# A graph layer on one core: bins made two blocks ahead, count matmuls first in a block, the last three tiles behind two groups of sums

## The chip, the core and the metric

The kernel runs on one core of one Trainium2 chip. The metric is device microseconds of one execution; the time before is the median of seven runs. A profile is one execution under the hardware profiler. Its engines are TensorE (PE, with its weight loads PEld), VectorE (DVE), ScalarE (ACT), GpSimd (POOL) and SyncE (SP), which issues most DMA transfers.

## What is computed

One message-passing layer over a graph of 6250 nodes and 206250 edges, sorted in the reference by `dst`; the kernel sums by `src`. Cut to what matters:

```python
msg  = concat([x[dst], edge_attr], 1)             # 64 + 64 features per edge
h    = relu(msg @ W1a.T + b1a)                    # 128 per edge
h    = h @ W1b.T + b1b                            # 64 per edge
sums = segment_sum(h, src, 6250); counts = segment_sum(1, src, 6250)
agg  = sums / max(counts, 1)
z    = relu(concat([x, agg], 1) @ W2a.T + b2a) @ W2b.T + b2b
y    = x + concat([z, x], 1) @ Wr.T + br
out  = layernorm(y)
```

## The kernel before

The edges are cut into 124 blocks of 13 tiles of 128 edges (`NGR`, `BLK`). A block goes through these steps; the line numbers are those of the kernel before.

- **Loads (`group`, SyncE).** The edge features (line 700) and the block's dst numbers relative to a window (`relt`, line 886) go into one of `EDGES` = 4 `rhs` buffers; 64 rows of the node table `ytab` go into `mv` (line 892).
- **`columns` (VectorE, line 898).** One comparison makes a one-hot of the dst numbers in the lower half of `rhs`.
- **`hidden` (TensorE, ScalarE).** 13 matmuls (line 912; in float32 each is two passes in the trace) into three PSUM buffers `h_ps`, in parts of 4, 3, 3 and 3 tiles, and a relu of each part (line 913) into one of `ROWS` = 6 `orow` buffers. Before the relus ScalarE writes the low bits of the src numbers into the same buffer (the "lo copy", line 1149), and for that the scatters that last read this buffer must have landed.
- **`bins_of` (VectorE, lines 811 to 818).** For each tile it marks which of 49 bins of 128 nodes each edge belongs to (`bins`) and counts the earlier ones by a scan (`had`). Each block continues the scan of the block before.
- **`counts_of` (TensorE, lines 831 and 832).** Four matmuls turn `bins` and `had` into places, in the only PSUM buffer `cnt_ps`.
- **`slots` (VectorE, lines 848 and 853).** A maximum over the bins and one more operation give `rowidx`, the row in DRAM for each edge.
- **`scatter` (GpSimd, line 919).** 13 indirect DMAs write the block's rows of `orow` to their places in `rows`, which is sorted by bins of nodes.
- **Sums.** From time to time a step's finished part of `rows` is read back: `issue` reads groups of at most three bins with up to 9 buffers `rt` (line 968, SyncE); `sum_next` makes a one-hot `oh` of the nodes (lines 994 and 997, VectorE) and multiplies (line 1015, TensorE), one group at a time, and adds an earlier group into `part` (line 1073). A read waits until the step's last block has landed; a step's reads begin four blocks after its end. `due` is the number of groups that are waiting to be summed when a block begins.

Blocks fall into five epochs (82, 17, 14, 7 and 4 blocks) with a buffer of rows each in turn. In the loop the order on TensorE, ScalarE, VectorE and SyncE is the program's order; GpSimd issues scatters alone. After the loop come the sums of the step before the last, and then, in an order made by a scheduler, the last step's sums and the node work, four bins at a time (lines 1225 to 1276).

In a block `k` the order was: bins of `k + 1`; loads of `k + 3`; the lo copy; the first ten tiles; reads; counts of `k + 1`; one group of sums; the last three tiles; the scatter; slots of `k + 1`; the other groups of sums; columns of `k + 2`.

Of the kernel before, what the change touches and what calls it, by code (L numbers as in the profile page):

```python
# [17 lines left out]
P = 128  # L18
# [440 lines left out]
SUMS, TILES = 3, 14  # L459
SEG = 25  # L460
PRE = 6
ROWS, EDGES, READS = 6, 4, 9
SPREAD = 4.8
EARLY = 14
CLEAR = 4
# [10 lines left out]
def fast_path(  # L476
# [201 lines left out]
    part = const.tile([P, NB, H + 1], F32, name="part")  # L678
    with (
        tc.tile_pool(name="orow", bufs=1) as op,  # L680
        tc.tile_pool(name="oh", bufs=2) as ohp,
        tc.tile_pool(name="node", bufs=4) as nodep,
        tc.tile_pool(name="cps", bufs=1, space=PSUM) as cpp,
        tc.tile_pool(name="slotp", bufs=1, space=PSUM) as slpp,
# [109 lines left out]
        def tiles_of(lo, hi_):  # L794

            t0 = lo
            while t0 < hi_:
                n = -(-(hi_ - t0) // -(-(hi_ - t0) // RD))
                yield t0, n
                t0 += n  # L800

        def bins_of(k):


            ep_ = epoch_of[k]
            c0 = k * BLK
            oh = slp.tile([P, 2 * HALF * T], BF16, name="bins")
            had = slp.tile([P, 2 * HALF * T], BF16, name="had")
            by_bin = oh.rearrange("p (b t) -> p b t", t=T)
            was = none_b if k == ep_.first else state["had"][:, :, BLK]  # L810
            nc.vector.tensor_tensor(by_bin[:, :, 0], was, on.rearrange("p (b t) -> p b t", t=T)[:, :, 1], op=ALU.mult)  # L811
            nc.vector.tensor_tensor(  # L812
                by_bin[:, :, 1:],
                ramp[:, : 2 * HALF, None].to_broadcast([P, 2 * HALF, BLK]),
                hi[:, None, c0 : c0 + BLK].to_broadcast([P, 2 * HALF, BLK]),
                op=ALU.is_equal,
            )
            nc.vector.tensor_tensor_scan(had, on, oh, 0.0, op0=ALU.mult, op1=ALU.add)  # L818
            oh, had = (v.rearrange("p (b t) -> p b t", t=T) for v in (oh, had))
            state["had"] = had  # L820
            return oh, had

        def counts_of(oh, had):
# [11 lines left out]
        def slots(k, ps):  # L835

            ep_ = epoch_of[k]
            c0 = k * BLK
            at = (k - ep_.first) % SEG * BLK
            if at == 0:  # L840
                m = min(ep_.end - k, SEG) * BLK
                state["bin"] = slp1.tile([P, SEG * BLK], F32, name="bin_at")[:, :m]
                nc.vector.tensor_scalar(
                    state["bin"], hi[:, c0 : c0 + m], float(STRIDE), -BIG, op0=ALU.mult, op1=ALU.add
                )
            v = ps[:, :, : HALF * T].rearrange("p i (b t) -> p i b t", t=T)
            row = slp.tile([P, T], F32, name="row")
            nc.vector.tensor_reduce(row, v.rearrange("p i b t -> p t i b"), axis=mybir.AxisListType.XY, op=ALU.max)  # L848

            def by_now(t):  # L850
                nc.vector.tensor_copy(t.rearrange("p (i b) -> p i b", i=2), v[:, :, :, BLK])

            s = nc.vector.scalar_tensor_tensor(
                rowidx[:, c0 : c0 + BLK], row[:, :BLK], BIG + STRIDE - 1,
                state["bin"][:, at : at + BLK], op0=ALU.min, op1=ALU.add,
            )
            state["slots"] = s.ins
            if k + 1 == EARLY:
                by_now(early)
                wrong(early, epochs[0].low, ALU.is_gt, slp)  # L860
            for st in ep_.steps[:-1]:
                if k + 1 == st.at:
                    full = slp1.tile([P, 2 * HALF], F32, name="full")
                    by_now(full)
                    wrong(full, st.hi, ALU.is_lt, slp)
            if k + 1 == ep_.end:
                by_now(ep_.tot)
                unused(ep_)

                if (ep_.end - ep_.first) * BLK > 255:  # L870
                    most = slp.tile([P, 2 * HALF], F32, name="most")
                    nc.vector.tensor_scalar(
                        most, state["had"][:, :, BLK], 255.5, None, op0=ALU.is_gt, op1=ALU.add,
                        accum_out=bad[:, state["bad"] :][:, :1],
                    )
                    state["bad"] += 1
# [18 lines left out]
        def columns(g):  # L895

            rhs, rel, _ = made[g]
            nc.vector.tensor_tensor(  # L898
                rhs[D:, :].rearrange("p (h e) -> p h e", h=2), rel,
                in_win[D:, :, None].to_broadcast([WIN, 2, NG * P // 2]), op=ALU.is_equal,  # L900
            )
# [3 lines left out]
        def hidden(k, parts):  # L905
            orow = orows[k % ROWS]
            rhs, _, m = made[k]
            for k0, n in parts:
                ps = hp.tile([P, SUB, H], F32, name="h_ps")
                for j in range(n):  # L910
                    c = k0 + j
                    nc.tensor.matmul(ps[:, j, :], rhs[:, c * P : (c + 1) * P], m, start=True, stop=True)  # L912
                nc.scalar.activation(orow[:, k0 : k0 + n, :H], ps[:, :n, :], AF.Relu)  # L913
# [224 lines left out]
        slots(0, counts_of(*bins_of(0)))  # L1138
        columns(0)
        columns(1)  # L1140
        for k, ep_ in enumerate(epoch_of):
            if k + 1 < NGR:
                ahead = bins_of(k + 1)

            if k + 3 < NGR:
                made[k + 3] = group(k + 3)
            due = len(issued) + len(marked) + len(to_issue)
            to_issue += groups_at[k]
            nc.scalar.copy(orows[k % ROWS][:, :, H + 1], lo[:, k * BLK : (k + 1) * BLK])  # L1149
            hidden(k, ((0, 4), (4, 3), (7, 3)))  # L1150
            if k == 0:
                bins(HEAD, NT)
                for i, o in enumerate((ALU.min, ALU.max)):
                    nc.vector.tensor_reduce(out_of[:NGR, i : i + 1], rel, axis=mybir.AxisListType.X, op=o)
            if k == 1:
                wn1b, wn2b = load(w1b, "wn1b"), load(w2b, "wn2b")
                b1b_c, b2b_c = column(b1b, "b1b_c"), column(b2b, "b2b_c")
                w2x_t = const.tile([D + 1, H], F32, name="w2x_t")
                nc.sync.dma_start(w2x_t[:D, :], w2aT[:D])
                nc.sync.dma_start(w2x_t[D:, :], b2a.rearrange("(o p) -> o p", o=1))  # L1160
                w2m_t = load(w2aT[D:], "w2m_t")
                wrz_t = load(wrT[:D], "wrz_t")
                wrx_t = const.tile([D + 1, D], F32, name="wrx_t")
                nc.sync.dma_start(wrx_t[:D, :], wrT[D:])
                nc.sync.dma_start(wrx_t[D:, :], br.rearrange("(o p) -> o p", o=1))
            if k == 4:


                wps = slpp.tile([P, P], F32, name="cnt_ps")
                nc.tensor.matmul(wps, wn1b, w2m_t, start=True, stop=True)  # L1170
                wam_t = const.tile([P, P], F32, name="wam_t")
                nc.vector.tensor_copy(wam_t, wps)
                wps = slpp.tile([P, D], F32, name="cnt_ps")
                nc.tensor.matmul(wps, wn2b, wrz_t, start=True, stop=True)
                wzz_t = const.tile([P, D], F32, name="wzz_t")
                nc.vector.tensor_copy(wzz_t, wps)
                nwzz_t = const.tile([P, D], F32, name="nwzz_t")
                nc.vector.tensor_scalar(nwzz_t, wps, -1.0, None, op0=ALU.mult)
                wps = slpp.tile([P, H + D], F32, name="cnt_ps")
                nc.tensor.matmul(wps[D : D + 1, :H], b1b_c, w2m_t, start=True, stop=True)  # L1180
                nc.tensor.matmul(wps[D : D + 1, H:], b2b_c, wrz_t, start=True, stop=True)
                nc.vector.tensor_add(w2x_t[D:, :], w2x_t[D:, :], wps[D : D + 1, :H])
                nc.vector.tensor_add(wrx_t[D:, :], wrx_t[D:, :], wps[D : D + 1, H:])
                nc.vector.tensor_add(wrx_t[:D, :], wrx_t[:D, :], ident[:D, :D])
            if 0 <= k - PRE < -(-NB // SUB):
                nodes_ahead((k - PRE) * SUB)
            if k in clears:
                clear(*clears[k])
            issue(k)
            if k + 1 < NGR:  # L1190
                ahead = counts_of(*ahead)

            if due > 0:
                sum_next()
                issue(k)
            hidden(k, ((10, 3),))
            made.pop(k)
            scatter(ep_, k)
            if k + 1 < NGR:
                slots(k + 1, ahead)  # L1200
            for _ in range(due - 1):
                sum_next()
                issue(k)
            if due == 0:
                collect(0)
            if k + 2 < NGR:
                columns(k + 2)
        for k in range(NGR, NGR + LATE):
            to_issue += groups_at[k]
            issue(k)  # L1210
# [164 lines left out]
```

## Time and profile before

| what | us |
|---|---|
| median of seven runs (lowest, highest) | 2213.67 (2211.32, 2215.72) |
| the profiled execution's own time | 2213.45 |
| its span, first to last instruction | 2211.7 |
| busy: POOL, PE, DVE, ACT | 1552.2, 1275.2, 1180.4, 311.0 |
| first and last start of a scatter | 58.3 and 2094.5 |

A line of the costliest groups reads: line, engine, operation, output and inputs, count, then busy time and mean ns of one, then the idle time of the engine just before these instructions and what ended it. A line of the waits reads: who waited, for what, the total in us, how often, the longest. A line of the timeline reads: start, length, engine, line, operation, tiles, and in brackets the idle time before it with what ended it; equal instructions that follow each other are put together (x20).

### The profile page before, as it was taken

What the parts mean: (1) busy time and instruction counts of PE and PEld (TensorE: products, weight loads), DVE (VectorE), ACT (ScalarE), POOL (GpSimd) and SP (SyncE); (2) the same over time, 40 slices, a digit from 0 to 9 for tenths busy, and PEclk for the clock granted to TensorE, in tenths of its full rate; (3) what the DMA queues carried; (4) which work ended last, traced back from release to release, by engine and by line L of the source; (5) the groups of instructions that cost most, each with busy time, mean ns of one, the idle gap of its engine ahead of it and who ended that gap; (6) DMA issues with size and microseconds to landing.
All of it is one profiled execution on the core that took longest, in us unless ns stands there. A gap on an engine that the chain in (4) does not pass through costs nothing.

```text
span 2211.7 us, 25263 instructions
## 1 busy us (share of the span) xinstructions
PE 1275.2 (58%) x8327; PEld 1193.9 (54%) x8327; DVE 1180.4 (53%) x2063; ACT 311.0 (14%) x791; POOL 1552.2 (70%) x1630
## 2 busy tenths in 40 slices
PE   4776543554536555365544765566664676486576
PEld 4665433554535544365544765566564576486465
DVE  2755342545427455165454755586754755384455
ACT  1221111111111111111111111111111111110034
POOL 1777777777777777777777777777777777777600
PEclk9877676777678676676776887777877878798798
DMA  5897575554445454354544856576655656476540
GB/s 151 263 343 222 148 197 169 174 153 139 135 135 161 140 152 134 111 171 133 158 138 130 235 152 207 150 212 179 181 166 163 202 170 203 143 228 204 169 116 20
DMA packets 199201, 373.66 MB, mean 169 GB/s; under 512 B 46362, under 2 KB 114908, under 8 KB 198932
## 3 DMA queue, kind: packets, MB, share of 16 engines
q1 hardware_dynamic: 115078, 218.90, 35.0%
q0 software_dynamic: 51584, 107.40, 15.4%
q10 hardware_dynamic: 32398, 45.65, 6.6%
q8 instruction: 68, 1.11, 0.2%
q14 instruction: 73, 0.60, 0.1%
HBM read 220.20 MB, written 151.59 MB: 168 GB/s over the span
## 4 chain that ended last, share of the span: by engine, by line
DMA 33%; POOL 26%; issue 16%; PE 12%; DVE 8%; ACT 2%; SPq 2%; ACTq 0%; POOLq 0%; DVEq 0%
POOL rows L919 26%; DMA rows<-orow,rowidx 25%; DMA rt<-rows 5%; PE sum_ps L1015 5%; PE h_ps L912 3%; DVE rhs L898 2%; DVE oh L997 2%; DVE had L818 1%; DMA rows<-padrow 1%; DMA rhs<-in_edgeT 1%; ACT orow L913 1%; PE h_ps L719 1%; PE h_ps L1245 1%; DMA mv<-ytab 1%; DVE bins L812 1%
## 5 line engine op out<-in xcount | busy, mean ns | idle before, releaser
L919 POOL DMA_INDIRECT rows<-orow,rowidx x1612 | 1544.4, 958 | 542.6 <-issue 403.2
L912 PE MATMUL h_ps<-mv,rhs 128*128 128x128 f32 x3224 | 549.3, 344 | 549.7 <-ACT orow L913 541.5
L912 PEld LDWEIGHTS h_ps<-mv,rhs 128*128 128x128 f32 x3224 | 526.0, 257 | 568.6 <-ACT orow L913 558.2
L1015 PE MATMUL sum_ps<-rt,oh 128*128 128x129 f32 x4006 | 553.7, 299 | 63.5 <-issue 28.1
L1015 PEld LDWEIGHTS sum_ps<-rt,oh 128*128 128x128 f32 x4006 | 542.0, 216 | 74.3 <-issue 48.0
L997 DVE TENSOR_TENSOR oh<-ramp,rt 128x512 f32<-128x512 f32 (+3 forms) x213 | 143.0, 702 | 497.0 <-DMA rt<-rows 455.9
L913 ACT ACTIVATE orow<-h_ps 128x512 f32<-128x512 f32 x496 | 233.0, 515 | 393.9 <-PE h_ps L912 365.2
L898 DVE TENSOR_TENSOR rhs<-rhs,ramp 64x1664 f32<-64x1664 bf16 x124 | 234.6, 1892 | 22.6 <-DMA rhs<-relt 19.3
L997 DVE TENSOR_TENSOR oh<-ramp,node 128x512 f32<-128x512 f32 (+3 forms) x237 | 187.1, 790 | 63.5 <-PE sum_ps L1015 53.4
L831 PE MATMUL cnt_ps<-had,one_w 128*128 128x350 bf16 x248 | 85.4, 350 | 216.5 <-DVE had L818 133.1
L1149 ACT CAST orow<-lo 128x13 f32<-128x13 bf16 x124 | 26.4, 213 | 1275.6 <-DMA rows<-orow,rowidx 1275.3
L818 DVE TENSOR_TENSOR_SCAN had<-ramp,bins 128x700 bf16<-128x700 bf16 x124 | 200.3, 1615 | 4.2
L848 DVE TENSOR_REDUCE row<-cnt_ps 128x14 f32<-128x700 f32 x124 | 109.2, 881 | 100.5 <-PE cnt_ps L832 99.8
L832 PEld LDWEIGHTS <-before_w 128*128 128x128 bf16 x248 | 26.4, 107 | 231.6 <-issue 221.6
L994 DVE SCALAR_TENSOR_TENSOR node<-unused,rt 128x4 f32<-128x4 bf16 (+3 forms) x237 | 37.6, 159 | 188.4 <-DMA rt<-rows 188.0
L812 DVE TENSOR_TENSOR bins<-ramp,hi 128x650 bf16<-128x650 f32 x124 | 108.2, 873 | 0.0
L832 PE MATMUL cnt_ps<-bins,before_w 128*128 128x325 bf16 x248 | 85.9, 351 | 0.0
L1073 DVE TENSOR_TENSOR part<-part,sum_ps 128x258 f32<-128x258 f32 (+2 forms) x166 | 76.5, 461 | 2.4 <-PE sum_ps L1015 2.4
L811 DVE TENSOR_TENSOR bins<-had,ramp 128x50 bf16<-128x50 bf16 x119 | 44.0, 370 | 3.0
L1116 PE MATMUL h_ps<-zT,w2x_t 65*128 65x512 f32 (+1 forms) x26 | 18.8, 814 | 37.0 <-ACT orow L913 37.0
L1121 DVE TENSOR_SCALAR zT<-h_ps 128x512 f32<-128x512 f32 (+1 forms) x13 | 8.5, 652 | 54.9 <-PE h_ps L1120 54.9
L1234 ACT ACTIVATE agg<-sum_ps,rc 128x128 f32<-128x128 f32 x49 | 17.0, 364 | 133.7 <-DVE node L994 106.6
(109 smaller groups left out, 438.6 us busy)
## 6 DMA issues: line engine op xcount, KB each, us to landing
rt<-rows SPq DMA_DIRECT2D x242, 260.0 KB
rhs<-in_edgeT SPq DMA_DIRECT2D x124, 416.0 KB
rt<-rows SPq DMA_DIRECT2D x106, 390.0 KB
rhs<-relt SPq DMA_DIRECT2D x124, 208.0 KB
rows<-orow,rowidx POOLq DMA_INDIRECT x1612
rows<-padrow ACTq DMA_DIRECT2D x4, 4680.0 KB
rows<-padrow ACTq DMA_DIRECT2D x8, 2340.0 KB
rt<-rows SPq DMA_DIRECT2D x48, 325.0 KB
```

The lines of the kernel that those rows point to most:

```text
L812: nc.vector.tensor_tensor(by_bin[:, :, 1:], ramp[:, : 2 * HALF, None].to_broadcast([P, 2 * HALF, BLK]), hi[:, None, c0 : c0 + BLK].to_broa ...
L818: nc.vector.tensor_tensor_scan(had, on, oh, 0.0, op0=ALU.mult, op1=ALU.add)
L831: nc.tensor.matmul(v, one_w, had[:, b, :], start=True, stop=False)
L832: nc.tensor.matmul(v[:, :, :BLK], before_w, oh[:, b, 1:], start=False, stop=True)
L848: nc.vector.tensor_reduce(row, v.rearrange("p i b t -> p t i b"), axis=mybir.AxisListType.XY, op=ALU.max)
L898: nc.vector.tensor_tensor(rhs[D:, :].rearrange("p (h e) -> p h e", h=2), rel, in_win[D:, :, None].to_broadcast([WIN, 2, NG * P // 2]), op= ...
L912: nc.tensor.matmul(ps[:, j, :], rhs[:, c * P : (c + 1) * P], m, start=True, stop=True)
L913: nc.scalar.activation(orow[:, k0 : k0 + n, :H], ps[:, :n, :], AF.Relu)
L919: s = nc.gpsimd.indirect_dma_start(out=ep_.rows, out_offset=bass.IndirectOffsetOnAxis(ap=rowidx[:, t : t + 1], axis=0), in_=orow[:, j, :], ...
L997: nc.vector.tensor_tensor(res[:, at_tile : at_tile + nb * n, :], ramp[:, None, :].to_broadcast([P, nb * n, P]), node[:, :, None].to_broadc ...
L1015: nc.tensor.matmul(of_bin(b), oh[:, at_tile, :], rt[:, j * n + t, : H + 1], start=t0 + t == st.lo[b] and not last, stop=t0 + t == st.hi[b] ...
L1073: nc.vector.tensor_add(to, to, g.ps[:, : g.nb, :])
```

## The change

The bins of block `k + 2` instead of `k + 1` are made in block `k`, so that the counts of `k + 1` can be the first matmuls of the block. VectorE's `columns` and `bins_of` for `k + 2` come ahead of the sums. The slots of `k + 1` follow the first group of sums, and the last three tiles and the scatter the second. A third one-hot buffer `oh` takes its space from the sixth `orow` buffer. Three products of weights in block 4 use `h_ps` in place of `cnt_ps`, which now holds counts across that place. `hads` keeps each block's `had`, since the newest one is no longer that of the block at hand.

```diff
-ROWS, EDGES, READS = 6, 4, 9
+ROWS, EDGES, READS = 5, 4, 9
...
-        tc.tile_pool(name="oh", bufs=2) as ohp,
+        tc.tile_pool(name="oh", bufs=3) as ohp,
...
+        hads = {}
...
-            state["had"] = had
+            state["had"] = hads[k] = had
...
-                        most, state["had"][:, :, BLK], 255.5, None, op0=ALU.is_gt, op1=ALU.add,
+                        most, hads[k][:, :, BLK], 255.5, None, op0=ALU.is_gt, op1=ALU.add,
...
         slots(0, counts_of(*bins_of(0)))
         columns(0)
         columns(1)
+        ahead = bins_of(1)
         for k, ep_ in enumerate(epoch_of):
-            if k + 1 < NGR:
-                ahead = bins_of(k + 1)
...
             nc.scalar.copy(orows[k % ROWS][:, :, H + 1], lo[:, k * BLK : (k + 1) * BLK])
+            if k + 1 < NGR:
+                counts = counts_of(*ahead)
             hidden(k, ((0, 4), (4, 3), (7, 3)))
+
+            if k + 2 < NGR:
+                columns(k + 2)
+                ahead = bins_of(k + 2)
             if k == 0:
                 bins(HEAD, NT)
...
-                wps = slpp.tile([P, P], F32, name="cnt_ps")
+                wps = hp.tile([P, P], F32, name="h_ps")
...
             issue(k)
-            if k + 1 < NGR:
-                ahead = counts_of(*ahead)
-
-            if due > 0:
-                sum_next()
-                issue(k)
-            hidden(k, ((10, 3),))
-            made.pop(k)
-            scatter(ep_, k)
-            if k + 1 < NGR:
-                slots(k + 1, ahead)
-            for _ in range(due - 1):
-                sum_next()
-                issue(k)
+
+            for i in range(max(due, 1)):
+                if due > 0:
+                    sum_next()
+                    issue(k)
+                if i == 0 and k + 1 < NGR:
+                    slots(k + 1, counts)
+                if i == min(1, max(due, 1) - 1):
+                    hidden(k, ((10, 3),))
+                    made.pop(k)
+                    scatter(ep_, k)
             if due == 0:
                 collect(0)
-            if k + 2 < NGR:
-                columns(k + 2)
```

More of the change, by code (lines that the diff above doesn't have):

```diff
@@ L1172, in fast_path @@
                 nc.vector.tensor_copy(wam_t, wps)
-                wps = slpp.tile([P, D], F32, name="cnt_ps")
+                wps = hp.tile([P, D], F32, name="h_ps")
                 nc.tensor.matmul(wps, wn2b, wrz_t, start=True, stop=True)
@@ L1178, in fast_path @@
                 nc.vector.tensor_scalar(nwzz_t, wps, -1.0, None, op0=ALU.mult)
-                wps = slpp.tile([P, H + D], F32, name="cnt_ps")
+                wps = hp.tile([P, H + D], F32, name="h_ps")
                 nc.tensor.matmul(wps[D : D + 1, :H], b1b_c, w2m_t, start=True, stop=True)
```

## The prediction

> **What bounds the kernel now.** I read the page first (busy time and costliest groups), then the table of waits, then the timeline of the start, of one stalled block and of the end.
>
> ```profile
> PE 1275.2 (58%) x8327; PEld 1193.9 (54%) x8327; DVE 1180.4 (53%) x2063; ACT 311.0 (14%) x791; POOL 1552.2 (70%) x1630
> ...
> L919 POOL DMA_INDIRECT rows<-orow,rowidx x1612 | 1544.4, 958 | 542.6 <-issue 403.2
> ```
>
> GpSimd issues 1612 scatters (13 for each of 124 blocks), 958 ns busy each and some 0.30 us between two. The 542.6 us of idle time are 1612 such pauses and one long wait:
>
> ```profile
> ACT orow L1149 <- DMA rows<-orow,rowidx: 1275.3, 105, 14.0
> ...
> DVE oh L997 <- DMA rt<-rows: 455.9, 62, 37.0
> ...
> POOL rows L919 <- ACT orow L913: 56.0, 21, 49.9
> ```
>
> Of the 56.0 us that scatters waited for ScalarE, 49.9 are the wait before the first one. ScalarE in turn waits 1275.3 us for old scatters to land: the engines in front run ahead of GpSimd until they have no free orow buffer. This is the start:
>
> ```profile
> 54.74 4.61 PE L912 MATMUL h_ps<-mv,rhs 128*128 128x128 f32 x20 [8.18 <-DMA mv<-ytab]
> ...
> 56.47 1.89 DVE L898 TENSOR_TENSOR rhs<-rhs,ramp 64x1664 f32<-64x1664 bf16 x1 [15.31 <-DMA rhs<-relt]
> ...
> 56.83 0.60 ACT L913 ACTIVATE orow<-h_ps 128x512 f32<-128x512 f32 x1 [9.90 <-PE h_ps L912]
> ...
> 58.29 1.13 POOL L919 DMA_INDIRECT rows<-orow,rowidx  x1 [49.87 <-ACT orow L913]
> 58.40 0.37 DVE L811 TENSOR_TENSOR bins<-had,ramp 128x50 bf16<-128x50 bf16 x1
> ...
> 59.46 1.61 DVE L818 TENSOR_TENSOR_SCAN had<-ramp,bins 128x700 bf16<-128x700 bf16 x1
> ...
> 61.13 0.45 PE L831 MATMUL cnt_ps<-had,one_w 128*128 128x350 bf16 x1 [1.77 <-DVE had L818]
> ...
> 62.25 5.33 PE L912 MATMUL h_ps<-mv,rhs 128*128 128x128 f32 x26
> 62.27 1.43 POOL L919 DMA_INDIRECT rows<-orow,rowidx  x1 [0.30 <-issue]
> ```
>
> And this a block in the middle (87) whose last three tiles were held up, with its first scatter below (two answers of the timeline), and the last scatter:
>
> ```profile
> 1407.49 0.21 ACT L1149 CAST orow<-lo 128x13 f32<-128x13 bf16 x1 [11.65 <-DMA rows<-orow,rowidx]
> ...
> 1427.64 0.49 ACT L913 ACTIVATE orow<-h_ps 128x384 f32<-128x384 f32 x1 [18.69 <-PE h_ps L912]
> ```
>
> ```profile
> 1488.40 0.95 POOL L919 DMA_INDIRECT rows<-orow,rowidx  x1 [0.30 <-DMA rows<-orow,rowidx]
> ```
>
> ```profile
> 2094.54 0.95 POOL L919 DMA_INDIRECT rows<-orow,rowidx  x1 [0.30 <-issue]
> ```
>
> From 58.29 to 2094.54 are 1611 steps, 1.264 us each: 0.958 busy, 0.30 pause. Nothing in front of GpSimd stops it for over 0.7 us in these 2036 us. So the execution is three pieces: 58.29 us until the first scatter, 2037.2 us of scatters, 116.2 us from 2095.49 to the end of the span, 2211.7; 1.75 us around it make its own time of 2213.45, 0.22 under the median of 2213.67. Only what moves the first scatter, opens a hole in the stream, or changes the last 116 us moves the time.
>
> **Counts first in a block (start).** TensorE's order in block 0 becomes: the counts of block 1, then the tiles of block 0. Those counts need bins and had of block 1, which VectorE makes after both calls of columns; the second waits for relt until 56.47. The SyncE order of the two built programs is the same, so this landing stays; had ends at 61.07 as now. Behind the waiting count matmuls stand all ten first tiles of block 0, their relus and with them the first scatter. TensorE starts the counts at 61.13 and the tiles at 62.25 instead of 54.74: 7.51 later. The first relu needs four tiles, eight passes: 8 x 4.61/20 = 1.84 us now, 8 x 5.33/26 = 1.64 at the place of the new start. So the first scatter moves by 7.3 to 7.5 us, to about 65.7. I take 7.4; nothing hides it, since GpSimd has nothing else to do.
>
> **Block 1 after that.** In front of rowidx of block 1 VectorE now has columns 1.89, bins and had 2.67 (58.40 to 61.07), the second bins call and the two reduces (60.99 to 67.17: 6.2) and slots 1.07: from 61.07 to about 73. There is one cnt_ps buffer, so the counts of block 2, again ahead of the tiles, wait for it: 74.0, the first relu of block 1 ends by 76.5. Its first scatter is due 16.6 to 17 us after block 0's (75.36 - 58.29 = 17.07 now), at 82.3 or later. 5.8 us in hand: nothing. If relt of block 2 landed only at 68.2, where it is first used without a wait now, 7.1 - 5.8 = 1.3 us would show; 0 is nearer, relt of block 1 took 3.57 us (52.88 to 56.45).
>
> **Steady blocks.** What the change removes is real: in block 87 TensorE waited 18.69 us in front of the last three tiles, behind counts whose had stood in VectorE's queue behind one-hots that waited for reads. But block 87's last relu ended at 1428.1 and its first scatter was issued at 1488.40: 60.3 us in hand. That is the smallest lead of any block from 11 on; the undisturbed ones have 77 to 78. (Blocks 2 to 10 build it up from 9.8 us; they and GpSimd now start equally later.) Removing the wait is worth 0. Moving columns and bins about on VectorE adds no instruction; TensorE has as many.
>
> **One orow buffer fewer.** The lo copy waits for the landing of block k-5 instead of k-6: the lead shrinks by one block, 13 x 1.264 = 16.4 us. The last three tiles come behind two groups of sums instead of one, a further 2.84 us (24 passes) to some 5; behind them queue the relu, the next lo copy, and SyncE's load into that block's rhs buffer. The worst lead becomes 60.3 - 16.4 - 5 = 39 us: 0. The read that a step starts with needs block k-5 too, so the front, now held one block longer, meets it landed more often; also 0. The three weight products of block 4 move from cnt_ps to h_ps, 0 under the same lead.
>
> **End.** With one block less of run-ahead the last blocks finish 16.4 us later, but the step before the last can't start before block 119 has landed (VectorE waited 20.6 us for it, until 2035.45), and TensorE stands idle from 2075 to 2103.1 for the final reads. 0 again. The third one-hot buffer: in the list of waits from 2098 on, no one-hot waits for TensorE, so it takes no wait away there. The built order differs in the last stretch only at its first and last bins: the sums of the last bins stand earlier, and the last transpose copy comes out from behind four y activations (1.43 us) and a 0.69 us wait for none. -2 at most, +0.5 if the earlier one-hot (0.95 us) holds up the first counts; I take -0.5, nearer to nothing because that copy's input, not the wait, is late in the trace.
>
> **A rule against it.** The scatter at 62.27 took 1.43 us beside VectorE's cast of hi (61.88 to 62.71), 0.47 too long; the one at 60.99 beside L664 took 0.98. The same operations now lie beside the first scatters again, so the net is 0. The Trainium skill (SBUF — State Buffer, Who interferes with whom) says that copies, casts and tensor_scalar on VectorE can take the port pair that it shares with GpSimd and block it for the whole instruction. By that, the three big operations (2.5 us) could cost up to 2.5 us, 1.9 more than now; the rows say 0.
>
> Sum: +7.4 + 0 - 0.5 = +6.9 on 2213.45 = 2220.35; with the 0.22 of the median, 2220.5.
>
> **Rivals.** (1) The end gives it back. TensorE is busy 77.8 of the last 109 us, so 31 us are there to win; the chain runs through 13 groups of four bins. If the third buffer saves 0.23 us in each, the loss falls to 4.4 us (0.2%, about what a measurement of this kernel can tell from no change); with 0.4 us the time is 2213.67 + 7.4 - 5.2 = 2215.9, no difference. Against it: no one-hot waits for TensorE there. (2) The same with a saving over 0.91 us in each group: 7.4 - 11.8 = -4.4, faster; at 1.1 us, 2206.8. Break-even is 0.57 us a group. The order of the two programs, the same in between, speaks against it. (3) GpSimd runs dry in the middle: a new stall of over 39 us eats the shorter lead, and every us above it is added. VectorE's longest wait for a read is 37.0 us, and that is already in the lead of 60.3. A stall of 47 us would give 2228.5. (4) The counts do not delay the first tiles: then 2213.2. The built order shows them in front.
>
> **Chances and range.** Forecast 0.80, (1) with (4) 0.11, (2) 0.04, (3) 0.05. So slower 0.85, same 0.11, faster 0.04. The forecast's own bounds are 7.3 - 2 = 5.3 and 7.5 + 1.3 + 0.5 = 9.3, that is 2219.0 to 2223.0; the medians themselves are uncertain by 1 to 2 us (the seven runs of before span 2211.32 to 2215.72). The range goes from 2216, into rival 1, to 2225, into rival 3.
>
> **What would show it.** First scatter near 65.7; the first L912 tiles behind the count matmuls at 62.25; last scatter near 2102; 115 to 116.5 us after it. Holes over 1 us between scatters speak for (3), a first scatter near 58 for (4), a tail under 109 us for (1) or (2).

## The result, and the profile after

The median of 15 runs of the changed kernel is 2220.56 us (2218.49 to 2222.75); the kernel before has 2213.67 us over 35 runs (2211.05 to 2216.82) on the same chip. The ratio is 1.003, with a 95% interval of 1.0024 to 1.0037: slower by 0.3%, 6.9 us, where 2220.5 us was forecast.

From the page of the kernel after, the group of the scatters. The line numbers of after are two higher than before in most places: L914, L915 and L921 are the tiles, the relus and the scatters; L833 and L834 the counts.

```profile
L921 POOL DMA_INDIRECT rows<-orow,rowidx x1612 | 1544.0, 958 | 550.4 <-issue 399.8
```

The same scatters take the same time; GpSimd's idle time in front of them has grown from 542.6 to 550.4 us. The waits of after say where:

```profile
ACT orow L1150 <- DMA rows<-orow,rowidx: 1484.4, 116, 16.3
...
ACT orow L915 <- PE h_ps L914: 209.8, 145, 17.2
...
POOL rows L921 <- ACT orow L915: 61.3, 15, 57.1
```

The wait before the first scatter is 57.1 us instead of 49.9. ScalarE's wait for tiles was, before,

```profile
ACT orow L913 <- PE h_ps L912: 365.2, 165, 18.7
```

and has fallen to 209.8 us, while its wait for old scatters to land has risen by as much and more. It looks as if the better order had freed the front (the engines ahead of GpSimd), which then stood longer at its gate; the buffers alone, below, correct this reading. The timeline of the start of after:

```profile
61.03 0.45 PE L833 MATMUL cnt_ps<-had,one_w 128*128 128x350 bf16 x1 [14.61 <-DVE had L820]
...
62.15 3.83 PE L914 MATMUL h_ps<-mv,rhs 128*128 128x128 f32 x26
...
64.00 1.16 ACT L915 ACTIVATE orow<-h_ps 128x512 f32<-128x512 f32 x2 [17.22 <-PE h_ps L914]
...
65.47 1.13 POOL L921 DMA_INDIRECT rows<-orow,rowidx  x1 [57.08 <-ACT orow L915]
...
66.36 0.86 DVE L665 CAST hi<-rt 128x1287 bf16<-128x1287 int32 x1
...
66.89 1.31 POOL L921 DMA_INDIRECT rows<-orow,rowidx  x1 [0.30 <-issue]
...
72.71 1.89 DVE L900 TENSOR_TENSOR rhs<-rhs,ramp 64x1664 f32<-64x1664 bf16 x1
...
73.56 0.96 POOL L921 DMA_INDIRECT rows<-orow,rowidx  x1 [0.30 <-issue]
...
75.59 0.60 ACT L915 ACTIVATE orow<-h_ps 128x512 f32<-128x512 f32 x1 [5.71 <-PE h_ps L914]
...
82.39 0.95 POOL L921 DMA_INDIRECT rows<-orow,rowidx  x1 [0.30 <-issue]
```

The tiles of block 0 begin behind the four count matmuls, at 62.15 instead of 54.74, and the first scatter starts at 65.47. The last line is the first scatter of block 1: its relu was done at 76.19, 6.2 us earlier. Block 87, which had waited 18.69 us for its last three tiles, and the last scatter, from the timeline of after:

```profile
1433.84 0.49 ACT L915 ACTIVATE orow<-h_ps 128x384 f32<-128x384 f32 x1 [1.04 <-PE h_ps L914]
```

```profile
2101.89 0.95 POOL L921 DMA_INDIRECT rows<-orow,rowidx  x1 [0.31 <-issue]
```

Block 87 now waits 1.04 us. Its first scatter is issued at 1495.80, 61.5 us after this relu; before, 60.3 us after it. Cut into the three pieces of the prediction, the two profiled executions are:

| us | before | after | difference |
|---|---|---|---|
| until the first scatter | 58.29 | 65.47 | +7.17 |
| first scatter to end of last | 2037.20 | 2037.38 | +0.18 |
| end of last scatter to end of span | 116.16 | 114.17 | -2.00 |
| span | 2211.66 | 2217.01 | +5.35 |

The profiled execution of after is one of its quickest (its own time is 2218.80); the medians differ by 6.9 us. The table is one execution against one, and its sum is 1.5 us under the medians' difference. The pieces of single executions scatter: with five or six `orow` buffers the stream of scatters took from 2036.6 to 2042.3 us in the profiled executions on the chips of the usual times. So what a change is worth is taken from the medians below, and the pieces say where it lies.

### The profile page after: what moved, and what is told of

It is laid out like the page before. It is cut to its first block, busy times and chain, and to the rows that moved or that the text cites. A ratio compares the mean times of both kernels' runs of the same rounds, so it can differ in the third digit from the quotient of the medians.

```text
span 2217.0 us, 25265 instructions
## 1 busy us (share of the span) xinstructions
PE 1297.3 (59%) x8327; PEld 1188.0 (54%) x8327; DVE 1183.1 (53%) x2063; ACT 309.5 (14%) x791; POOL 1551.8 (70%) x1629
## 4 chain that ended last, share of the span: by engine, by line
DMA 38%; POOL 28%; issue 16%; PE 7%; DVE 7%; SPq 2%; ACT 2%; POOLq 0%; ACTq 0%; DVEq 0%
DMA rows<-orow,rowidx 29%; POOL rows L921 28%; DMA rt<-rows 5%; PE h_ps L914 2%; DMA rhs<-relt 2%; DVE oh L999 2%; PE sum_ps L1017 2%; DVE rhs L900 1%; DMA rhs<-in_edgeT 1%; DVE had L820 1%; DMA rows<-padrow 1%; ACT orow L915 1%; PE h_ps L719 1%; PE h_ps L1247 1%; PE h_ps L1251 1%
## 5 line engine op out<-in xcount | busy, mean ns | idle before, releaser
L921 POOL DMA_INDIRECT rows<-orow,rowidx x1612 | 1544.0, 958 | 550.4 <-issue 399.8
L914 PE MATMUL h_ps<-mv,rhs 128*128 128x128 f32 x3224 | 588.8, 354 | 702.1 <-ACT orow L915 696.8
L914 PEld LDWEIGHTS h_ps<-mv,rhs 128*128 128x128 f32 x3224 | 565.2, 266 | 738.4 <-ACT orow L915 717.0
L1017 PE MATMUL sum_ps<-rt,oh 128*128 128x129 f32 x4006 | 496.4, 281 | 57.3 <-DVE part L1075 44.8
L1017 PEld LDWEIGHTS sum_ps<-rt,oh 128*128 128x128 f32 x4006 | 480.9, 198 | 60.5 <-DVE part L1075 46.6
L915 ACT ACTIVATE orow<-h_ps 128x512 f32<-128x512 f32 x496 | 230.6, 514 | 210.5 <-PE h_ps L914 209.8
L833 PE MATMUL cnt_ps<-had,one_w 128*128 128x350 bf16 x248 | 117.1, 473 | 36.2 <-DVE had L820 14.6
L834 PE MATMUL cnt_ps<-bins,before_w 128*128 128x325 bf16 x248 | 118.0, 476 | 0.0
L834 PEld LDWEIGHTS <-before_w 128*128 128x128 bf16 x248 | 35.2, 142 | 63.2 <-issue 41.2
L833 PEld LDWEIGHTS <-one_w 128*128 128x128 bf16 x248 | 35.8, 144 | 16.1
```

Source lines behind the costliest of these rows:

```text
L833: nc.tensor.matmul(v, one_w, had[:, b, :], start=True, stop=False)
L834: nc.tensor.matmul(v[:, :, :BLK], before_w, oh[:, b, 1:], start=False, stop=True)
L921: s = nc.gpsimd.indirect_dma_start(out=ep_.rows, out_offset=bass.IndirectOffsetOnAxis(ap=rowidx[:, t : t + 1], axis=0), in_=orow[:, j, :], ...
L1017: nc.tensor.matmul(of_bin(b), oh[:, at_tile, :], rt[:, j * n + t, : H + 1], start=t0 + t == st.lo[b] and not last, stop=t0 + t == st.hi[b] ...
```

## The experiments

Every ratio is to the kernel before, run in turn on the same chip. Two of the chips took about a fifth longer for every kernel of this case, the kernel before included; times from there are set only against times from the same chip.

**The start undone alone.** The kernel after, with the counts of block 1 behind the first ten tiles in block 0 and nowhere else:

```diff
-            if k + 1 < NGR:
+            if 0 < k and k + 1 < NGR:
                 counts = counts_of(*ahead)
             hidden(k, ((0, 4), (4, 3), (7, 3)))
+            if k == 0:
+                counts = counts_of(*ahead)
```

> The changed kernel with one thing undone: in block 0 alone the counts of block 1 come behind the first ten tiles again. Theory (the loss is the late first scatter): the first scatter goes from 65.5 us back to 58.3, the stream stays at 2037 us, the time falls by 7.2 us from 2220.6 to 2213.4, no different from before (or up to 2 us under it, if the shorter end of the profiled execution, 114.2 for 116.2 us, is no accident). Rival (the loss comes from the order inside the steady blocks or from the five orow buffers): 2220 stays.

Measured: 2215.04 us (11 runs), ratio 0.9997 (0.9988 to 1.0006). Its timeline:

```profile
59.04 1.13 POOL L921 DMA_INDIRECT rows<-orow,rowidx  x1 [50.65 <-ACT orow L915]
...
76.64 0.60 ACT L915 ACTIVATE orow<-h_ps 128x512 f32<-128x512 f32 x1 [5.71 <-PE h_ps L914]
...
77.98 0.96 POOL L921 DMA_INDIRECT rows<-orow,rowidx  x1 [1.71 <-issue]
```

The first scatter is back at 59.04, and with it the loss is gone in the medians: within the interval, one line's place in one of 124 blocks is the whole cost of the change. Not all of it comes back. GpSimd now stands still for 1.71 us, 1.4 over its pause, in front of the first scatter of block 1, whose relu ended at 77.23. Moved 6.4 us forward, the stream of scatters has used up the 6.2 us that block 1 had in hand in the kernel after; the relu itself ended 1.0 us later here than there. The stream as a whole took 2042.24 us in this execution, not the 2037 expected: this hole is 1.4 us of that, another of 1.8 us comes before the 220th scatter, and the execution is 2.1 us over its median. Block 1's tiles stand behind the counts of block 2, and these behind VectorE's chain, as the prediction's working for block 1 has it.

**The start done alone.** The kernel before, with the counts ahead of the tiles in block 0 only:

```diff
             nc.scalar.copy(orows[k % ROWS][:, :, H + 1], lo[:, k * BLK : (k + 1) * BLK])
+            if k == 0:
+                ahead = counts_of(*ahead)
             hidden(k, ((0, 4), (4, 3), (7, 3)))
...
-            if k + 1 < NGR:
+            if 0 < k and k + 1 < NGR:
                 ahead = counts_of(*ahead)
```

> The kernel before with one part of the change: in block 0 alone the counts of block 1 come ahead of the first ten tiles; six orow buffers, two one-hot buffers, all other blocks as before. Theory: first scatter at 65.5 instead of 58.3, time 2213.7 + 7.2 = 2220.9. Rival (steady blocks or buffers): 2213.7. If the end gains from the third one-hot buffer, this kernel has no such gain and is above the changed kernel by that much (0 to 2 us).

Measured: 2223.95 us (6 runs), ratio 1.0034 (1.0022 to 1.0046). Its timeline:

```profile
61.70 0.45 PE L831 MATMUL cnt_ps<-had,one_w 128*128 128x350 bf16 x1 [14.55 <-DVE had L818]
...
62.82 6.23 PE L912 MATMUL h_ps<-mv,rhs 128*128 128x128 f32 x46
...
66.15 1.13 POOL L919 DMA_INDIRECT rows<-orow,rowidx  x1 [57.72 <-DVE out_of L1156]
```

The lead of the other blocks (from the end of a block's last relu to its first scatter) stays at 77.6 us (median of blocks 11 and later), the start is 7.9 us later, and the whole loss is there, 7.5 us by the ratio.

**The buffers alone.** The kernel before with the two sizes of the change:

```diff
-ROWS, EDGES, READS = 6, 4, 9
+ROWS, EDGES, READS = 5, 4, 9
...
-        tc.tile_pool(name="oh", bufs=2) as ohp,
+        tc.tile_pool(name="oh", bufs=3) as ohp,
```

> The kernel before with five orow buffers and three one-hot buffers, its order untouched. Theory: first scatter at 58.3, the lead of GpSimd's queue shrinks by 16.4 us to a median of 61 and a minimum above 40 with no hole in the stream, time 2213.7, or up to 2 us less by the end's order. Rival (a shorter lead opens holes): each us of hole is added, 2216 or more.

Measured: 2214.41 us (11 runs), ratio 0.9993 (0.9984 to 1.0002). The waits, and the last relu of block 87 in the timeline:

```profile
ACT orow L1149 <- DMA rows<-orow,rowidx: 1479.8, 117, 15.8
...
ACT orow L913 <- PE h_ps L912: 187.5, 137, 9.8
```

```profile
1433.88 0.49 ACT L913 ACTIVATE orow<-h_ps 128x384 f32<-128x384 f32 x1 [3.04 <-PE h_ps L912]
```

The median lead falls by 16.3 us, to 61.3, one block of 13 x 1.264 = 16.4 us, and that costs nothing that the medians show. These lines also correct a reading of the waits above. The sixth buffer taken away brings ScalarE's wait for tiles down from 365.2 to 187.5 us and its wait for landings up to 1479.8 us, with the old order of the work. A fall of the one and a rise of the other is what a shorter lead looks like; it isn't proof that a better order did it. The same holds for block 87. With six buffers ScalarE waits 13.9 to 18.7 us for the last three tiles in seven of the blocks from 11 on; with five and the old order it waits 3.04 us in block 87 and nowhere from block 11 on over 5.23, with five and the new order 1.04 and at most 4.17. With two `orow` buffers, the old order and still two one-hot buffers (next experiment) it is at most 4.95. So a front that is held longer loses these stalls by itself, and the new order takes some 2 us more off block 87. VectorE's longest wait for a read falls with them, from 37.0 to 20.4 us.

One thing in the stream does go with five buffers: in four of the five such kernels profiled on the chips of the usual times GpSimd stands still for 1.9 to 2.1 us, 1.6 to 1.8 over its pause, before the 220th scatter, with no wait that the profile names. With six or two buffers and in the kernel with the earlier start, below, it does not. Its cause is open, and the median of the buffers alone shows no loss by it.

**A lead of less than one block.** Both kernels with two `orow` buffers, so that the front can run only some 12 us ahead:

```diff
-ROWS, EDGES, READS = 6, 4, 9        # before
+ROWS, EDGES, READS = 2, 4, 9
...
-ROWS, EDGES, READS = 5, 4, 9        # after
+ROWS, EDGES, READS = 2, 4, 9
```

> The kernel before with two orow buffers instead of six: the lead of the front over GpSimd shrinks by four blocks of 16.4 us, from 77.6 in the middle to 12 us. If the wait in front of the last three tiles is real (block 87: a lead of 60.3, 17 less than the others), some blocks now stop GpSimd: holes of 5 to 20 us in all, ratio to the kernel before 1.002 to 1.010. If the lead is elastic (ScalarE held back at the lo copy costs nothing later): no holes over 3 us beyond the first 400 us, ratio 0.999 to 1.002.

> The changed kernel with two orow buffers instead of five: the lead shrinks by three blocks, from 61.4 to 12 us, as in the run of the kernel before with two. If the change removes the wait in front of the last three tiles, this run has fewer and shorter holes than that one: at most 5 us in all, and its ratio to the kernel before is 1.003 (the later start less the shorter end) to 1.005. If the two groups of sums ahead of the last three tiles cost as much as the wait they replace: holes of 5 to 20 us here too, ratio 1.005 to 1.013.

Measured: 2229.72 us for before (4 runs), ratio 1.0067 (1.005 to 1.0084), and 2229.67 us for after (4 runs), ratio 1.0058 (1.0041 to 1.0074). The median lead is 12.1 us in both. Holes in the stream, which the first theory of each wanted or allowed, did not come; and the second missed the end. GpSimd's waits in the kernel before with two buffers are

```profile
POOL rows L919 <- issue: 402.2, 1317, 0.6
...
POOL rows L919 <- ACT orow L913: 53.5, 12, 50.2
```

and beside the wait for the first scatter none is over 0.6 us (1.1 in after with two). The long stalls of the last three tiles are gone as well, as with five buffers, so a lead of 12 us has none of them to cover. The loss is at the end: 132.67 us after the last scatter for before with two buffers and 124.26 for after, against 116.16 and 114.17. TensorE's timeline at the end, first of before, then of before with two buffers:

```profile
2067.42 7.58 PE L1015 MATMUL sum_ps<-rt,oh 128*128 128x129 f32 x60 [0.16 <-PE sum_ps L1015]
...
2103.10 4.21 PE L1015 MATMUL sum_ps<-rt,oh 128*128 128x129 f32 x18 [28.09 <-issue]
```

```profile
2111.82 7.59 PE L1015 MATMUL sum_ps<-rt,oh 128*128 128x129 f32 x60 [0.17 <-PE sum_ps L1015]
```

The x60 line is the last of the step before the last. With two buffers it ends at 2119.41 instead of 2075.00, which is 45.3 us later against the end of the last scatter (2094.57 and 2095.49). The 28.1 us in which TensorE waited for the last reads cover that much of it, and 45.3 - 28.1 = 17.2 us are left; the end grew by 16.5. The same sum for after with two buffers: 41.4 us later against its last scatter, 29.7 covered, 11.7 left, 10.1 measured. So the front's lead is worth nothing in the middle and is spent at the end, and there the cover was large enough for one buffer (16.4 us) but not for three or four. The changed kernel loses some 6 us less at this place, which its later start takes back: the two kernels measure the same. Whether its order or its third one-hot buffer saves them was not tried.

The same two were also run on a chip of the longer times.

> The kernel before with two orow buffers instead of six: what are its stalls worth when the cover is gone? From its trace: the median lead of 77.6 us falls by four blocks, 65.7 us, to 11.9; eight blocks have leads 12.8 to 17.5 us under the median, so holes of 0.7 to 5.4 us, 20 us together, open in the stream: 2234. Rival: the engines in front, held by the buffers, come later to the reads, which have landed by then; the stalls vanish, no holes, 2214.

> The changed kernel with two orow buffers. From its trace: median lead 61.4 - 49.3 = 12.1 us, the lowest from block 11 on 48.9 - 49.3 = -0.4 (during the clears of the first blocks); so next to no holes, 7 us for the late start, 2220 to 2222, some 13 us faster than the old order with two buffers: what the change removes, seen without its cover. Rival (stalls vanish in both, or the three tiles behind two groups of sums open holes of their own): no faster than the old order with two buffers, 2221 or more.

Measured there, with 2652.43 us for the kernel before: 2654.56 us (10 runs), ratio 1.0011 (0.9993 to 1.0029), and 2638.81 us (4 runs), ratio 0.9938 (0.9914 to 0.9963). The conditions of the expectations did not hold on that chip, so they are neither met nor missed. On the usual chips, above, it went as their rivals have it in the stream: no stalls and no holes to speak of in either, and no difference. Lines of the waits of before with two buffers there:

```profile
PE h_ps L912 <- issue: 506.1, 357, 14.3
...
POOL rows L919 <- ACT orow L913: 267.4, 65, 50.1
```

TensorE stands 506.1 us in front of tiles while it waits for nothing that the profile shows; on the chips of the usual times that row is not among its long waits. The tiles come late, and GpSimd waits for relus 65 times: the median lead is -12.6 us, and the front is the bound. The changed kernel gains here, 2638.81 against 2654.56, but not in the blocks. In the profiled executions its first scatter comes 8.1 us later, the stream takes 2426.87 against 2425.77 us, and the whole gain is the end after the last scatter, 145.15 against 161.86 us. So even where the front is the bound, the new order does not quicken the stream; and as on the usual chips, order and third one-hot buffer were not separated in the end.

**The third one-hot buffer taken back.** The kernel after with two:

```diff
-        tc.tile_pool(name="oh", bufs=3) as ohp,
+        tc.tile_pool(name="oh", bufs=2) as ohp,
```

> The changed kernel with two one-hot buffers instead of three. If the third buffer is what shortens the end: section from the 10th to the 13th output transfer 14 to 16 us (12.4 with three), time from the last scatter to the end of the span 115.5 to 117 us, ratio to the kernel before 1.0035 to 1.005. If the order of the end does it: section 12.4 us, tail 113.5 to 114.5, ratio 1.0030. First scatter at 65.5 either way.

Measured: 2224.49 us (5 runs), ratio 1.0038 (1.0024 to 1.0052); the end is 115.98 us long, and from the 10th to the 13th output transfer 15.4 us pass, 12.4 in after and 16.2 in before. On a chip of the longer times:

> The changed kernel with two one-hot buffers instead of three, all else kept. Theory (the end is shorter, 114.2 for 116.2 us, because a third buffer lets the scheduler put the last bins' sums earlier): the end goes back to 116 us or more and the median to 2222 to 2223 (on the chip of the first comparison). Rival (the shorter end is an accident of TensorE's clock in one execution): end of 114 us or either, median as the changed kernel's.

2652.02 us there (12 runs), ratio 1.0005 (0.9989 to 1.0021), and 14.1 us between those transfers, 12.4 in after with two `orow` buffers. That stretch is 12.38 us in all eight kernels profiled with three one-hot buffers and 14.15 to 16.22 in all six with two, whatever the rest. So it is the buffer, through the order that the scheduler makes of the end with it, that shortens this stretch. Over the chips of the usual times the ends are 116.16, 115.98 and 117.07 us with two one-hot buffers and six or five `orow` buffers (before, this kernel, the start done alone), and 114.17, 113.99, 113.18 and 115.30 with three (after, the start undone alone, the kernel below, the buffers alone). Where the 2 us lie is seen in the last 17 matmuls, those of the last two groups of bins. Windows of before, of this kernel, of the start done alone, and of after; the columns are length, then busy time of PE, PEld, DVE, ACT and POOL, then the granted clock, the DMA share and GB/s:

```profile
2196.65:2203.80 7.15, 5.58 (x17) 3.23 (x16) 2.67 (x13) 0.93 (x3) 0.00 (x0) 0.52 0.09 23
```

```profile
2210.20:2216.45 6.25, 4.70 (x17) 3.10 (x16) 2.68 (x13) 0.93 (x3) 0.00 (x0) 0.67 0.11 26
```

```profile
2206.70:2211.90 5.20, 3.40 (x17) 2.01 (x16) 2.56 (x13) 0.92 (x3) 0.00 (x0) 0.95 0.12 32
```

```profile
2203.50:2208.70 5.20, 3.42 (x17) 2.30 (x17) 3.87 (x27) 2.66 (x8) 0.00 (x0) 1.00 0.13 28
```

The same 17 matmuls, the first four in another order with three one-hot buffers, take 7.15 us at a granted clock of 0.52, 6.25 at 0.67 and 5.20 at 0.95 or 1.00. (The windows are cut by up to 0.2 us; from the first one's start to the last one's end it is 7.30 us before and 5.13 in after.) Before, they began 100.95 us after the last scatter, in after 100.71, and ended at 108.25 and 105.83. Of these 2.4 us the rest of the end gives back 0.4, which leaves the 2.00. In the start done alone, with two one-hot buffers, they run at nearly the full clock but begin at 103.70; in the buffers alone, with three, they run at 1.00 and begin at 102.08, so that its end is only 0.9 us shorter than before. Why two buffers give either a late start of this piece or a low clock in it was not settled.

**A version without the loss.** The start undone alone left ScalarE's queue in view. In after its four loads of `mv` stand in front of the copies of the node table that everything waits for. This kernel has them issued by GpSimd, which is idle then:

```diff
-    for m in mv:
-        nc.scalar.dma_start(m[:D, :], w1aT[D:])
...
+    for m in mv:
+        nc.gpsimd.dma_start(m[:D, :], w1aT[D:])
```

> block0_back with the four loads of mv issued by GpSimd, which is idle from 8 to 58 us, instead of ScalarE, whose queue stands still from 16.7 to 26.9 us in front of them, so that the copies of the node table start late (28.6 us). If the time is first scatter + 2037 + end, the node table is done 7 us earlier, the first scatter comes near 51 us and the time falls to 2213.4 - 7 = 2206, faster than both kernels. If the start is held by something else (transfers that share the DMA engines), the first scatter stays at 56 to 58 and the time at 2212 to 2213.

Measured: 2206.52 us (5 runs), ratio 0.9954 (0.994 to 0.9967): quicker than both kernels. ScalarE in after, and then ScalarE and GpSimd in this kernel:

```profile
16.40 10.37 ACTq L632 DMA_DIRECT2D mv<-in_W1a  x4
...
28.46 1.55 ACT L720 COPY part<-h_ps 128x512 f32<-128x512 f32 x3
```

```profile
18.07 0.59 ACT L720 COPY part<-h_ps 128x512 f32<-128x512 f32 x1 [10.53 <-PE h_ps L719]
...
52.16 1.03 POOL L921 DMA_INDIRECT rows<-orow,rowidx  x1 [41.45 <-ACT orow L915]
```

The copies begin 10.4 us earlier than in after, and the first scatter comes 6.9 us earlier than in the start undone alone, all of it kept: the two medians differ by 8.5 us. (In the profiled executions the stream and the end are 2.9 and 0.8 us shorter too.) The hole in front of the first scatter of block 1 is 1.4 us here as well. Two additions to it were tried on chips of the longer times only. In the first, columns and bins of block 2 come in block 0 only after the slots of block 1:

```diff
-            if k + 2 < NGR:
+            if 0 < k and k + 2 < NGR:
                 columns(k + 2)
                 ahead = bins_of(k + 2)
...
                     slots(k + 1, counts)
+                    if k == 0:
+                        columns(2)
+                        ahead = bins_of(2)
```

> early_start, and in block 0 VectorE makes the columns and bins of block 2 only after the slots of block 1, so that these come 4.6 us sooner. early_start has a hole of 1.4 us ahead of block 1's first scatter (its 14th). Theory: this hole goes, 1.4 us less than early_start, 2205. If the hole had another cause (ScalarE's copy of lo) it stays.

In the second the node features come in four parts instead of two as well:

```diff
-    half = NB // 2 * P
-    nc.scalar.dma_start(zT[:D, :half], xT[:, :half])
-    nc.scalar.dma_start(zT[:D, half:N], xT[:, half:])
+    cuts = [0, 8 * P, 20 * P, 34 * P, N]
+    for c0, c1 in zip(cuts, cuts[1:]):
+        nc.scalar.dma_start(zT[:D, c0:c1], xT[:, c0:c1])
```

> early_block1 with the node features loaded in four growing parts instead of two halves, so that TensorE's first tiles of the node table need 8 of 49 column blocks. In early_start TensorE begins at 16.0 us with the first half. If that transfer's size sets the begin, it comes near 10 us, the node table is done 4 to 6 us earlier, the first scatter near 47 and the time near 2200. If the transfers on the SyncE queue, which share the DMA engines, set it, or the landing of relt (39.3 us) becomes the bound, it gains 0 to 3 us.

Measured: 2624.43 us (5 runs), ratio 0.9886 (0.9869 to 0.9903), and 2598.82 us (6 runs) against 2634.91 on another such chip, ratio 0.9883 (0.9855 to 0.9912). The wait before block 1's first scatter did not go; it is 3.03 and 2.71 us. The trace of the first shows why, on the other chip: the slots of block 1 are done 3.9 us sooner (62.91, 66.77 in the kernel with the earlier start), but the scan of block 2, `had`, now ends behind them at 67.54, and the counts of block 2, which stand ahead of block 1's tiles, begin at 67.60 instead of 66.61. The first scatter comes at 52.87 and 53.37: the four parts bring nothing at the start. TensorE begins at 14.06 with them instead of 15.78, and then waits for a further part until 19.79. Both kernels gain over the kernel before there, but how much of that is theirs and how much the earlier start's was not taken apart.

## Why the prediction held, step by step

- **Counts first in block 0.** Expected: the tiles from 62.25 and the first scatter 7.3 to 7.5 us later. Measured: 62.15 and 7.17, just under. The step was shown both ways: done alone it costs 7.5 us, undone alone it takes the loss away.
- **Block 1.** Expected: relu done by 76.5, scatter due at 82.3, 5.8 us in hand, cost 0. Measured: 76.19, 82.39, 6.2. The 1.3 us for a late `relt` did not come. That the margin is real is shown by the 1.4 us hole when the start moves 6.4 us forward.
- **Steady blocks and one buffer fewer.** Expected: 0, with a worst lead of 39 us. Measured: +0.18 us over the whole stream, and a worst lead of 48.9 (block 11). The 39 came from taking 16.4 and 5 us from block 87's old lead, but the wait that made that lead short was gone: 61.5 us there now. The prediction credits the reordering with removing that wait; the buffers alone show that one `orow` buffer fewer removes most of it, 18.69 to 3.04 us, which the prediction names (the read is met landed more often) and prices at 0. The cost of 0 was right by the medians, for the kernel with the buffers alone too; the hole before the 220th scatter is in the +0.18.
- **End.** Expected: -0.5, at most -2. Measured: -2.00 in the profiled execution. This is the term that was mis-sized, and the end of 114.17 us lies under the 115 to 116.5 given as its sign. The prediction read the end by the order of the work and held the third buffer to be worth nothing, since no one-hot waited for TensorE there. It took the last matmuls at the durations of before, and these were the durations of a clock of 0.52. That the sum still fell on the median to 0.1 us is in part luck: in the executions profiled 7.17 + 0.18 - 2.00 is 5.35, the medians say 6.9, and their own uncertainty is 1 to 2 us.
- **The rule against it.** The scatter at 66.89 took 1.31 us beside the cast of `hi` at 66.36, 0.35 over the usual 0.96; the one at 73.56 took 0.96 beside the 1.89 us comparison of line 900. All scatters together are 0.5 us over that length in after and 0.8 before. The term of 0 holds. The cast was not alone, though: the long scatter ends at 68.21, 0.12 us behind the operation of line 666 (67.26 to 68.09), as it does before (63.70 and 63.58), which looks like a wait for that operation. By the Trainium skill (SBUF — State Buffer, Who interferes with whom) such a wait can last the whole instruction, by their durations an estimate of up to 2.5 us for the three; the most that a run here shows is about 1 us, two scatters of 1.60 and 1.28 us in the kernel with the earlier start.
- **Rivals.** The end did give something back, but not 0.23 us in each of 13 groups: all but 0.25 us of it is behind the first 101 us, in the last two. GpSimd never ran dry in the middle; after's longest idle time behind the first scatter is 1.9 us. And the counts did delay the first tiles.

## What to carry to other kernels

Find the engine whose stream never stops, and cost a change by what it does before the first and after the last instruction of that stream; a wait removed in an engine that runs ahead only comes back at its gate, and before an order is credited with removing it, run the buffer sizes alone. When a reordering is right for the steady state, write the first iteration separately: here block 0 had nothing to hide the reordering behind, and one condition on `k` takes the loss away. Before a wait is held to be gone, ask in the trace whether it only moved to the next gate, and whether the lead that now seems spare is spent after the loop.

## What the runs showed of the hardware

- The granted clock went with the length of the end's last piece: the same 17 matmuls took 7.15 us at 0.52 and 5.20 at 1.00, on the critical chain, with the rest of the last 116 us at 0.92 and 0.90.
- A queue of DMA issues is a place on the path. Four small loads held ScalarE's queue for 10.37 us in front of copies whose input was ready; issued elsewhere, the first scatter came 6.9 us earlier.
- On two of the chips used, TensorE stands for 506.1 us (the kernel before with two `orow` buffers) and 313.4 us (the node features in four parts) in front of its tiles without any wait that the profile names, the kernel before is a fifth longer, and the bound moves from GpSimd to the front. A verdict from one chip need not hold on another: the changed kernel with two one-hot buffers is 0.38% slower on a usual chip and no different from before on one of these (1.0005).
